# Half of a similarity matrix by transposes, and a second image prepared at another time: an attention and scan kernel on one Trainium2 core

## The chip, the cores and the metric

The kernel runs on one core of a Trainium2 chip. The time is device microseconds of one execution; the time of a version is the median of its runs. The core has five engines that work through queues of their own: PE (TensorE, matrix products; "PEld" is its weight load), DVE (VectorE), ACT (ScalarE), POOL (GpSimd) and SP (SyncE, which here only issues transfers). They wait for one another by semaphores. An engine takes its instructions in order, so an instruction that waits holds up all that stand behind it.

## What is computed

Eight images x of 256 channels and 48 x 48 = 2304 positions go through two layers. Each layer normalizes its input in groups of eight channels (`_gn`), and the result is added to the input.

```python
# layer 0
feat_pos = tokens @ W.T + bias
feat = feat_pos[:, :, :c]
pos = feat_pos[:, :, c:]
...
pos = pos / jnp.maximum(norm, 1e-12)
sim = jnp.einsum('bnc,bmc->bnm', pos, pos)
topksim, topkid = jax.lax.top_k(sim, K)
topkfeat = jax.vmap(lambda f, idx: f[idx])(feat, topkid)
attn = jax.nn.softmax(topksim, axis=-1)
out = jnp.einsum('bnk,bnkc->bnc', attn, topkfeat)
```

K is 16. The matrix sim (2304 x 2304 for each image) is symmetric. Layer 1 is a state-space model, twice in a row (DEPTH = 2): a layer norm, a projection, a convolution of four taps, SiLU, step sizes by softplus, and the recurrence

```python
dA = jnp.exp(dt_t[:, :, None] * A)
h = h * dA + dt_t[:, :, None] * B_t[:, None, :] * x_t[:, :, None]
y = jnp.einsum('bds,bs->bd', h, C_t)
```

over all 2304 positions, for 512 inner channels and 16 states, then a gate and a projection back.

## The kernel before

**Two streams.** Layer 0 of an image is a Python generator, `layer0` (L230 to L522), that issues a little work and then yields. Layer 1 is one long list of slots (L991 to L1008). The first image's layer 0 runs alone (L528); the Tile framework may reorder instructions there. From `manual_schedule` (L545) on, the order of issue is the order of the program. There, each slot m issues its share of layer 1 and then calls `ahead.go(m)` (L1008, L977), which takes one step of the next image's `layer0`. So image 1's layer 0 runs beside image 0's layer 1, and so on; the last image's layer 1 has no company.

**Layer 1.** A unit is one chunk of 384 positions at one depth; an image has 12 units, and a unit has 32 slots, so an image has 384. A slot holds one scan step: ACT makes decays (`decay`, L820, one slot ahead), POOL products `bx` (`make_bx`, L797, for two slots), DVE the scan (`run_scan`, L832), and DVE or POOL the product with C. Two hand-made tables, `between` and `behind` (L929, L943), give the slot, relative to the unit's first scan, of all else: for instance `load_v` at -42, `affine` and `mean` at -37, `center` at -35, `normal` at -22 (it makes vn), `in_proj` 0 at -21, `x_proj` at -13. Entries of `between` are issued before the slot's scan, those of `behind` after it. The slots begin at -42. `load_v` of an image first calls `ahead.finish` (L971), which issues whatever is left of that image's layer 0 in one piece; image 1's `load_v` is in slot 12 x 32 - 42 = 342.

**Layer 0.** First statistics: six chunks xs of x are loaded (L251, L264), DVE makes `bn_stats` (L261), and `group_stats` (L182) turns these into rstd and shift in eight steps, through PE, ACT and POOL. The weights w0 (512 KB) are loaded after the first chunks (L255). Then each chunk is loaded a second time (xt, L267 and L278), ACT normalizes it (L280), PE projects it (pp, L310, to pos; pf, L319, to feat), and pos is scaled by its inverse norm. Then come 18 blocks of 128 rows, by the table `within` (L500), 16 steps apart: `similar` (L394, five pieces psim of up to 512 columns, each two matmuls), `keep_similar` (L404, ACT copies them to sim), `top` (L410, DVE: maximum of eight, replace, maximum, replace), `others` (L432, ACT: rest), `turn` (L439, PE transposes sim and subtracts the rest), `weights` (L451, ACT: exp, aT), `weigh` (L459, PE: po), `average` (L469, ACT: o), `turn_back` (L478, PE: pr), `finish` (L486, DVE adds x and makes statistics; x1 is stored). `within` starts at -9 and its last step is 17 x 16 + 24 = 296, so there are 306 steps, and eight more of `group_stats`. Before its first block the generator yields `begin`, which is -9 (L515). `go` then waits until `(m + 1 - PHASE - begun) % BLOCK == 0` (L986, PHASE 6, BLOCK 16), so that image 1's blocks keep a fixed phase against layer 1's slots.

**Constants.** ACT issues 28 small loads at the start (L121 to L152) and then takes the exp of A_sb (L153). After image 0's layer 0, DVE makes the diagonal matrices dg of D_param (L540), and they are stored to memory (L541), for `load_d` (L687).

Of the kernel before, what the change touches and what calls it, by code (L numbers as in the profile page):

```python
# [8 lines left out]
F32 = mybir.dt.float32  # L9
BF16 = mybir.dt.bfloat16  # L10
AF = mybir.ActivationFunctionType
# [4 lines left out]
P = 128  # L16
# [9 lines left out]
def tile_conv_preact(  # L26
# [41 lines left out]
    BLOCK = 16  # L68
    TOPK = (1, 10)
    PHASE = 6  # L70


    SHARE = ("GGVGGGVVGGGGGGVG", "GGGVGVVGVVVGVGVG", "VGVGVGVVGGVVGGVG")
# [62 lines left out]
    for d in range(DEPTH):  # L136
        xp = xp_wT[d].rearrange("(k p) e -> p k e", p=P)

        nc.scalar.dma_start(xp_sb[:, d, :, d * RB : d * RB + R], xp[:, :, 0:R])
        nc.scalar.dma_start(xp_sb[:, d, :, R - d * R : E - d * R], xp[:, :, R:E])  # L140
        nc.scalar.dma_start(dtp_sb[d * RB : d * RB + R, :], dtp_wT[d])
        nc.scalar.dma_start(nw[:, d], norm_w[d].rearrange("(k p) -> p k", p=P))
        nc.scalar.dma_start(nbias[:, d], norm_b[d].rearrange("(k p) -> p k", p=P))
        nc.scalar.dma_start(cw[:, d], conv_w[d].rearrange("(k p) t -> p k t", p=P))
        nc.scalar.dma_start(cbias[:, d], conv_b[d].rearrange("(k p) -> p k", p=P))
        nc.scalar.dma_start(dtb[:, d], dtp_b[d].rearrange("(k p) -> p k", p=P))
        nc.scalar.dma_start(dpar[:, d], D_param[d].rearrange("(k p) -> p k", p=P))
        for j in range(J):
            nc.scalar.dma_start(
                A_sb[j * G : (j + 1) * G, d],  # L150
                A_log[d].rearrange("(i g) s -> g i s", g=G)[:, :, j * Q : (j + 1) * Q],
            )  # L152
    nc.scalar.activation(A_sb, A_sb, AF.Exp)  # L153

    nc.vector.tensor_scalar(A_sb, A_sb, LEAST, -1.0, ALU.max, ALU.mult)

    h_st = const.tile([P, DEPTH, STEPS, Q], F32, tag="h_st", name="h_st")
    tail = const.tile([P, DEPTH, CB, H], F32, tag="tail", name="tail")

    def rsqrt_start(r, var, eps):  # L160

# [20 lines left out]
    def group_stats(st, found, mm0, name):  # L182


        mv = small.tile([P, CB, 2], F32, tag="gn_mv", name=f"mv_{name}")
        for cb in range(CB):
            nc.vector.bn_aggr(mv[:, cb, :], st[:, cb])
# [5 lines left out]
        nc.scalar.copy(mean, pm)  # L193
# [18 lines left out]
        nc.gpsimd.tensor_scalar(shift, shift, -1.0, None, ALU.mult)  # L212
        found.extend((rstd, shift))
        yield
# [12 lines left out]

    def layer0(b, left, pool, ps0, alone):  # L230
        def mm0(w, name):
            return ps0.tile([P, 512], F32, tag="mm", name=name, bufs=5 if alone else 3)[:, :w]
# [11 lines left out]
        def leave_psum():  # L244
# [1 line left out]
                made, use = pending.pop(0)  # L246
                use(made)

        st = small.tile([P, CB, NCH, 6], F32, tag="gn_st0", name=f"st0_{b}")
        xs = {  # L250
            c: load_chunk(pool, x[b], c, "x", f"xs_{b}_{c}", 3 * more) for c in range(2 * more)  # L251
        }
# [5 lines left out]
        for c in range(NCH):  # L258
            xt = xs.pop(c)
            for cb in range(CB):  # L260
                nc.vector.bn_stats(st[:, cb, c, :], xt[:, cb, :])  # L261
            n = c + 2 * more
            if n < NCH:
                xs[n] = load_chunk(pool, x[b], n, "x", f"xs_{b}_{n}", 3 * more)  # L264
            yield
        found = []
        nxt = load_chunk(pool, x[b], 0, "x", f"xt_{b}_0", 3 * more)  # L267
        yield from group_stats(st, found, mm0, f"a{b}")
        rstd, shift = found
        pos = pool.tile([P, CB, N], F32, tag="pos", name=f"pos_{b}", bufs=1)  # L270
        feat = pool.tile([P, NB, C], F32, tag="feat", name=f"feat_{b}", bufs=1)
        loaded = {0: nxt}
        n2, rn = {}, {}

        def normalized(c):
            xn = loaded.pop(c)
            if c + 1 < NCH:
                loaded[c + 1] = load_chunk(pool, x[b], c + 1, "x", f"xt_{b}_{c + 1}", 3 * more)  # L278
            for cb in range(CB):
                nc.scalar.activation(  # L280
                    xn[:, cb, :], xn[:, cb, :], AF.Identity,
                    bias=shift[:, cb : cb + 1], scale=rstd[:, cb : cb + 1],
                )
            return xn
# [106 lines left out]
        PT = 4  # L391
        blocks = [{} for _ in range(NB)]

        def similar(t, i):  # L394

            c0, w = widths[i]
            pm = blocks[t]["psim", i] = mm0(w, f"psim_{b}_{t}_{i}")
            for k in range(CB):
                nc.tensor.matmul(  # L399
                    pm, pos[:, k, t * P : (t + 1) * P], pos[:, k, c0 : c0 + w],  # L400
                    start=(k == 0), stop=(k == CB - 1),
                )

        def keep_similar(t, i):  # L404
            c0, w = widths[i]
            if i == 0:
                blocks[t]["sim"] = pool.tile([P, N], F32, tag="sim", name=f"sim_{b}_{t}", bufs=2)
            nc.scalar.copy(blocks[t]["sim"][:, c0 : c0 + w], blocks[t].pop(("psim", i)))  # L408

        def top(t, i):  # L410

# [110 lines left out]
        left.update(x1=x1, rstd=found[0], shift=found[1])  # L522

    lefts = [{} for _ in range(B)]
    with tc.tile_pool(name="first", bufs=1) as pool0, tc.tile_pool(
        name="first_ps", bufs=1, space=PSUM
    ) as ps0:
        for _ in layer0(0, lefts[0], pool0, ps0, True):  # L528
            pass

    diag = hbm.tile([P, DEPTH, DC + 1, DB, P], F32, tag="diag", name="diag", bufs=1)
    with tc.tile_pool(name="setup", bufs=2) as setup:
        for d in range(DEPTH):
            for t in range(DC, DC + 1):
                dg = setup.tile([P, DB, P], F32, tag="dg", name=f"dg_{d}_{t}")
                for k in range(DB):
                    f = cw[:, d, k, t : t + 1] if t < DC else dpar[:, d, k : k + 1]
                    nc.vector.tensor_scalar(dg[:, k], ident, f, None, ALU.mult)  # L540
                nc.sync.dma_start(diag[:, d, t], dg)  # L541
# [144 lines left out]

    def load_d(unit, k):  # L687
        unit["dmat"][k] = keep.tile([P, P], F32, tag="dmat", name=f"dmat_{unit['u']}_{k}")
        nc.sync.dma_start(unit["dmat"][k], diag[:, unit["d"], DC, k])

    def tap(unit, e):
        d = unit["d"]
# [267 lines left out]
    class Ahead:  # L960
# [26 lines left out]

# [62 lines left out]
```

## Time and profile before

| what | us |
|---|---|
| runs | 9895.0 to 9908.42, median of 4: 9903.97 |
| the profiled execution | 9895.45 |
| its span | 9893.7 |
| first MAX8 (top) of image 0 | 88.3 |
| last block's MAX8 of image 0 | 415.3 |
| first scan (slot 0) | 521.4 |
| first scan of the last image | 8819.7 |

Over the span DVE is busy for 8958.5 us (91%), POOL for 8943.4 (90%), PE for 8001.0 (81%) and ACT for 7326.8 (74%). These shares mix stages with different limits, so they are read by stage. In the profile's group lines stand the line of the kernel, the engine, the operation, the tile written and the tiles read, and the shape; in a timeline, the start and the duration come first, and in square brackets the idle time of the engine before the instruction and what ended it. "SPq" and "ACTq" are issues of transfers. Matmul records overlap, because PE is pipelined; the distance of their starts is what one costs.

### The profile page before, as it was taken

What the parts mean: (1) busy time and instruction counts of PE and PEld (TensorE: products, weight loads), DVE (VectorE), ACT (ScalarE), POOL (GpSimd) and SP (SyncE); (2) the same over time, 40 slices, a digit from 0 to 9 for tenths busy, and PEclk for the clock granted to TensorE, in tenths of its full rate; (3) what the DMA queues carried; (4) which work ended last, traced back from release to release, by engine and by line L of the source; (5) the groups of instructions that cost most, each with busy time, mean ns of one, the idle gap of its engine ahead of it and who ended that gap; (6) DMA issues with size and microseconds to landing.
All of it is one profiled execution on the core that took longest, in us unless ns stands there. A gap on an engine that the chain in (4) does not pass through costs nothing. (4 is left out here: it accounts for less than half of the span.)

```text
span 9893.7 us, 133780 instructions
## 1 busy us (share of the span) xinstructions
PE 8001.0 (81%) x36736; PEld 4381.5 (44%) x36736; DVE 8958.5 (91%) x7993; ACT 7326.8 (74%) x15966; POOL 8943.4 (90%) x3927
## 2 busy tenths in 40 slices
PE   8888887788878888788877888788887788866665
PEld 6644544444534454344444445344544444422222
DVE  4589998999989999899998999889998999988998
ACT  4477787778777877777777787777777778766766
POOL 0089999999989999899998999999998999999999
PEclk9989998899988998899988999889998899977777
DMA  1144445444444444544454444444445444444544
GB/s 32 37 132 124 137 129 152 123 131 128 137 137 134 126 139 132 144 121 140 126 151 126 134 125 138 142 133 122 137 126 155 119 135 126 140 136 130 144 140 121
DMA packets 1243503, 1271.37 MB, mean 129 GB/s; under 512 B 266592, under 2 KB 1215840, under 8 KB 1242752
## 3 DMA queue, kind: packets, MB, share of 16 engines
q1 hardware_dynamic: 1230496, 1262.45, 45.1%
q8 instruction: 293, 4.80, 0.2%
q14 instruction: 458, 3.75, 0.1%
q10 hardware_dynamic: 12256, 0.36, 0.1%
HBM read 1048.94 MB, written 212.86 MB: 128 GB/s over the span
## 5 line engine op out<-in xcount | busy, mean ns | idle before, releaser
L804 POOL TENSOR_TENSOR bx<-BC,dtxr 128x1536 f32<-128x1536 f32 x1536 | 5304.3, 3457 | 115.6 <-PE y L889 56.0
L828 ACT ACTIVATE da<-dtr,A_sb 128x385 f32<-128x385 f32 x6144 | 3594.9, 585 | 867.7 <-DVE bx L843 558.9
L843 DVE TENSOR_TENSOR_SCAN bx<-da,bx 128x770 f32<-128x770 f32 x2040 | 3523.6, 1747 | 188.3 <-ACT da L828 140.9
L871 POOL TENSOR_TENSOR bx<-bx,BC 128x1536 f32<-128x1536 f32 (+1 forms) x1320 | 3308.8, 2507 | 213.7 <-DVE bx L843 203.6
L843 DVE TENSOR_TENSOR_SCAN da<-da,bx 128x770 f32<-128x770 f32 x1032 | 1809.3, 1753 | 189.4 <-ACT da L828 144.6
L602 PE MATMUL pe<-vn,inw 128*128 128x384 f32 (+1 forms) x3072 | 1249.9, 539 | 393.5 <-DVE xr L924 87.7
L399 PE MATMUL psim<-pos 128*128 128x512 f32 (+1 forms) x2880 | 1371.0, 608 | 182.2 <-ACT sim L408 75.2
L465 PE MATMUL po<-feat,aT 128*128 128x256 f32 x5184 | 1362.2, 412 | 14.4 <-ACT aT L454 7.5
L889 PE MATMUL y<-bx,sel 128*32 128x384 f32 x12288 | 1226.7, 534 | 44.4 <-POOL bx L871 33.9
L465 PEld LDWEIGHTS po<-feat,aT 128*128 128x128 f32 x5184 | 1027.1, 205 | 362.0 <-issue 112.1
L845 DVE TENSOR_TENSOR bx<-da,BC 128x768 f32<-128x768 f32 x1032 | 989.2, 958 | 35.5
L602 PEld LDWEIGHTS pe<-vn,inw 128*128 128x128 f32 x3072 | 585.6, 205 | 902.6 <-issue 184.0
L399 PEld LDWEIGHTS psim<-pos 128*128 128x128 f32 x2880 | 552.7, 206 | 817.4 <-issue 468.2
L889 PEld LDWEIGHTS y<-bx,sel 128*32 128x32 f32 x12288 | 394.8, 118 | 862.4 <-issue 734.4
L702 DVE SCALAR_TENSOR_TENSOR xc<-pe,cw,xc 128x384 f32<-128x384 f32 x1152 | 696.4, 611 | 43.1 <-ACT xc L694 15.9
L732 PE MATMUL pd<-dbl,dtp_sb 16*128 16x384 f32 x768 | 426.9, 672 | 338.2 <-ACT dt L741 206.1
L859 ACT COPY h_st<-da 128x2 f32<-128x2 f32 x832 | 131.8, 158 | 685.4 <-DVE bx L845 679.3
L454 ACT ACTIVATE aT<-pt 128x512 f32<-128x512 f32 (+1 forms) x720 | 388.4, 549 | 246.7 <-PE pt L446 240.4
L445 PE MATMUL pt<-ident,sim 128*128 128x128 f32 x2592 | 538.0, 290 | 38.9 <-DVE v L666 22.1
L907 PE MATMUL pw<-z,ow 128*128 128x384 f32 x1536 | 527.9, 496 | 14.2 <-DVE v L666 7.5
L437 ACT ACTIVATE rest<-left,three 128x512 bf16<-128x512 f32 (+1 forms) x720 | 467.2, 671 | 59.4 <-DVE left L422 59.4
L446 PE MATMUL pt<-minus,rest 128*128 128x128 bf16 x2592 | 489.9, 224 | 3.3 <-ACT rest L437 3.2
(146 smaller groups left out, 9777.8 us busy)
## 6 DMA issues: line engine op xcount, KB each, us to landing
dtxr<-dtx_d SPq DMA_DIRECT2D x6144, 48.0 KB, 1.8
dtr<-dt_d SPq DMA_DIRECT2D x6144, 48.0 KB, 1.8
BC<-bc_d SPq DMA_DIRECT2D x768, 192.0 KB, 3.8
inw<-in_in_wT_dram SPq DMA_DIRECT2D x768, 128.0 KB, 2.2
dtx_d<-dtx SPq DMA_DIRECT2D x384, 192.0 KB, 2.0
dt_d<-dt SPq DMA_DIRECT2D x384, 192.0 KB, 2.2
ow<-in_out_wT_dram SPq DMA_DIRECT2D x96, 512.0 KB, 3.9
dmat<-diag SPq DMA_DIRECT2D x384, 64.0 KB, 2.3
```

What stands on the lines that cost most here:

```text
L399: nc.tensor.matmul(pm, pos[:, k, t * P : (t + 1) * P], pos[:, k, c0 : c0 + w], start=(k == 0), stop=(k == CB - 1),)
L445: nc.tensor.transpose(pt[:, q], row["sim"][:, r], ident)
L465: nc.tensor.matmul(row["po"], aT[:, m % PT, :], feat[:, m, :], start=(m == 0), stop=(m == NB - 1))
L602: nc.tensor.matmul(pe, w[:, k], unit["vn"][:, k, lo:], start=(k == 0), stop=(k == CB - 1))
L702: nc.vector.scalar_tensor_tensor(unit["xc"][e], unit["pe"][e][:, k : k + T], cw[:, unit["d"], e, k : k + 1], unit["xc"][e], ALU.mult, ALU.add,
L804: nc.gpsimd.tensor_tensor(bx[:, :, 1:], unit["BC"][0], unit["dtxr"][i].unsqueeze(1).to_broadcast([P, Q, T]), ALU.mult,)
L828: nc.scalar.activation(da[:, s * (1 + T) : (s + 1) * (1 + T)], unit["dtr"][i], AF.Exp, scale=A_sb[:, unit["d"], i, p * HQ + s : p * HQ + s ...
L843: nc.vector.tensor_tensor_scan(h, da, g, 0.0, ALU.mult, ALU.add)
L845: nc.vector.tensor_tensor(bx[:, :, 0:T], da.rearrange("p (q t) -> p q t", q=HQ)[:, :, 1:], unit["BC"][1][:, qs], ALU.mult,)
L871: nc.gpsimd.tensor_tensor(g[:, :, 0:T], g[:, :, 1:], unit["BC"][1][:, qs], ALU.mult)
L889: nc.tensor.matmul(y[j * G : (j + 1) * G, :], sel, unit["bx"][k * J + j][:, q, 0:T], start=False, stop=True, skip_group_check=True,)
L907: nc.tensor.matmul(pw, unit["ow"][:, k, cb * P : (cb + 1) * P], unit["z"][k], start=(k == 0), stop=(k == DB - 1),)
```

## The change

- **Similarities of image 0** (`alone`): for row block t, column blocks left of the diagonal are no longer multiplied. `keep_similar` also has POOL copy the part right of the diagonal into a new tile `tri`; `similar` transposes the copies of rows m < t into place and multiplies only from the diagonal on. The other images multiply as before.
- **Constants**: their 26 loads go from ACT's queue to SP's, and are issued after image 0's group statistics and the load of w0. The exp of A_sb and the matrices dg follow there, ahead of the first normalization in program order. The separate stage that made dg after layer 0 is gone.
- **Input chunks of image 0** are all loaded at once, kept in six buffers, and not loaded a second time.
- **Image 1's input statistics** are made during image 0's blocks, one step every fourth slot. Its layer 0 then starts in slot -20 (`EARLY`) instead of -42, and has fewer steps: it lacks the 14 of the statistics.
- **Images 2 to 7**: w0 is loaded ahead of the first two chunks rather than after them; the first second load of x is issued after the statistics, one step ahead of its normalization, and there is one step more before the blocks.

```diff
+    EARLY = -20
...
-        nc.scalar.dma_start(xp_sb[:, d, :, d * RB : d * RB + R], xp[:, :, 0:R])
...
+    def scan_constants():
+        for d in range(DEPTH):
...
+            nc.sync.dma_start(xp_sb[:, d, :, d * RB : d * RB + R], xp[:, :, 0:R])
...
+        nc.scalar.activation(A_sb, A_sb, AF.Exp)
+
+        nc.vector.tensor_scalar(A_sb, A_sb, LEAST, -1.0, ALU.max, ALU.mult)
...
+    known = {}
+
+    def input_stats(b, pool, mm0, ahead, kept):
+        bufs = NCH if kept is not None else 3
+        st = small.tile([P, CB, NCH, 6], F32, tag="gn_st0", name=f"st0_{b}")
+        xs = {c: load_chunk(pool, x[b], c, "x", f"xs_{b}_{c}", bufs) for c in range(ahead)}
+        yield
+        for c in range(NCH):
+            xt = xs.pop(c)
+            for cb in range(CB):
+                nc.vector.bn_stats(st[:, cb, c, :], xt[:, cb, :])
+            n = c + ahead
+            if n < NCH:
+                xs[n] = load_chunk(pool, x[b], n, "x", f"xs_{b}_{n}", bufs)
+            if kept is not None:
+                kept[c] = xt
+            yield
+        found = []
+        yield from group_stats(st, found, mm0, f"a{b}")
+        known[b] = found
...
+        if alone:
+            loaded = {}
+            yield from input_stats(b, pool, mm0, 6, loaded)
+        else:
+            loaded = {0: None}
         w0_t = pool.tile([P, N], F32, tag="left", name=f"w0_{b}", bufs=more)
         w0_sb = w0_t[:, 0 : CB * 2 * C].rearrange("p (k o) -> p k o", k=CB)
         nc.sync.dma_start(w0_sb, w0T.rearrange("(k p) o -> p k o", p=P))
...
+        if not alone:
+            if b not in known:
+                yield from input_stats(b, pool, mm0, 2, None)
+            loaded[0] = load_chunk(pool, x[b], 0, "x", f"xt_{b}_0", 3)
+        yield
+        rstd, shift = known[b]
...
+        if alone:
+            tri = pool.tile([P, NB * (NB - 1) // 2 * P], F32, tag="tri", name="tri", bufs=1)
+
+        def above(t, m, n):
+            at = t * NB - t * (t + 1) // 2 + m - t - 1
+            return tri[:, at * P : (at + n) * P]
+
         def similar(t, i):
 
             c0, w = widths[i]
             pm = blocks[t]["psim", i] = mm0(w, f"psim_{b}_{t}_{i}")
+            if alone:
+                for m in range(c0 // P, min(t, (c0 + w) // P)):
+                    nc.tensor.transpose(pm[:, m * P - c0 : (m + 1) * P - c0], above(m, t, 1), ident)
+                lo = max(c0, t * P)
+                if lo < c0 + w:
+                    for k in range(CB):
+                        nc.tensor.matmul(
+                            pm[:, lo - c0 :], pos[:, k, t * P : (t + 1) * P], pos[:, k, lo : c0 + w],
+                            start=(k == 0), stop=(k == CB - 1),
+                        )
+                return
...
             nc.scalar.copy(blocks[t]["sim"][:, c0 : c0 + w], blocks[t].pop(("psim", i)))
+            lo = max(c0, (t + 1) * P)
+            if alone and lo < c0 + w:
+                nc.gpsimd.tensor_copy(
+                    above(t, lo // P, (c0 + w - lo) // P), blocks[t]["sim"][:, lo : c0 + w]
+                )
...
         yield begin
+        other = input_stats(1, pool, mm0, 6, {}) if alone and B > 1 else iter(())
         for m in range(begin, max(parts) + 1):
+            if m >= 0 and m % 4 == 0:
+                next(other, 0)
...
+        run = layer0(0, lefts[0], pool0, ps0, True)
+        while 0 not in known:
+            next(run)
+        scan_constants()
+        for d in range(DEPTH):
+            dg = pool0.tile([P, DB, P], F32, tag="dg", name=f"dg_{d}", bufs=1)
+            for k in range(DB):
+                nc.vector.tensor_scalar(dg[:, k], ident, dpar[:, d, k : k + 1], None, ALU.mult)
+            nc.sync.dma_start(diag[:, d], dg)
+        for _ in run:
             pass
...
         def go(self, m):
-            if self.image == B:
+            if self.image == B or m < EARLY:
                 return
```

More of the change, by code (lines that the diff above doesn't have):

```diff
@@ L135, in tile_conv_preact @@
     A_sb = const.tile([P, DEPTH, STEPS, Q], F32, tag="A_sb", name="A_sb")
-    for d in range(DEPTH):
-        xp = xp_wT[d].rearrange("(k p) e -> p k e", p=P)
-        nc.scalar.dma_start(xp_sb[:, d, :, d * RB : d * RB + R], xp[:, :, 0:R])
[L140 to L152, printed above, removed]
@@ L153, in tile_conv_preact @@
-    nc.scalar.activation(A_sb, A_sb, AF.Exp)
-    nc.vector.tensor_scalar(A_sb, A_sb, LEAST, -1.0, ALU.max, ALU.mult)
     h_st = const.tile([P, DEPTH, STEPS, Q], F32, tag="h_st", name="h_st")
     tail = const.tile([P, DEPTH, CB, H], F32, tag="tail", name="tail")
+    def scan_constants():
+        for d in range(DEPTH):
+            xp = xp_wT[d].rearrange("(k p) e -> p k e", p=P)
+            nc.sync.dma_start(xp_sb[:, d, :, d * RB : d * RB + R], xp[:, :, 0:R])
+            nc.sync.dma_start(xp_sb[:, d, :, R - d * R : E - d * R], xp[:, :, R:E])
+            nc.sync.dma_start(dtp_sb[d * RB : d * RB + R, :], dtp_wT[d])
+            nc.sync.dma_start(nw[:, d], norm_w[d].rearrange("(k p) -> p k", p=P))
+            nc.sync.dma_start(nbias[:, d], norm_b[d].rearrange("(k p) -> p k", p=P))
+            nc.sync.dma_start(cw[:, d], conv_w[d].rearrange("(k p) t -> p k t", p=P))
+            nc.sync.dma_start(cbias[:, d], conv_b[d].rearrange("(k p) -> p k", p=P))
+            nc.sync.dma_start(dtb[:, d], dtp_b[d].rearrange("(k p) -> p k", p=P))
+            nc.sync.dma_start(dpar[:, d], D_param[d].rearrange("(k p) -> p k", p=P))
+            for j in range(J):
+                nc.sync.dma_start(
+                    A_sb[j * G : (j + 1) * G, d],
+                    A_log[d].rearrange("(i g) s -> g i s", g=G)[:, :, j * Q : (j + 1) * Q],
+                )
+        nc.scalar.activation(A_sb, A_sb, AF.Exp)
+        nc.vector.tensor_scalar(A_sb, A_sb, LEAST, -1.0, ALU.max, ALU.mult)
@@ L247, in leave_psum @@
                 use(made)
[L249 to L252, printed above, removed]
+        if alone:
[3 more added lines that the diff above has]
+            loaded = {0: None}
         w0_t = pool.tile([P, N], F32, tag="left", name=f"w0_{b}", bufs=more)
@@ L256, in layer0 @@
         sq = w0_t[:, CB * 2 * C : CB * 2 * C + CB * T].rearrange("p (k t) -> p k t", k=CB)
+        if not alone:
+            if b not in known:
+                yield from input_stats(b, pool, mm0, 2, None)
+            loaded[0] = load_chunk(pool, x[b], 0, "x", f"xt_{b}_0", 3)
         yield
[L258 to L269, printed above, removed]
+        rstd, shift = known[b]
         pos = pool.tile([P, CB, N], F32, tag="pos", name=f"pos_{b}", bufs=1)
         feat = pool.tile([P, NB, C], F32, tag="feat", name=f"feat_{b}", bufs=1)
-        loaded = {0: nxt}
         n2, rn = {}, {}
@@ L276, in normalized @@
             xn = loaded.pop(c)
-            if c + 1 < NCH:
-                loaded[c + 1] = load_chunk(pool, x[b], c + 1, "x", f"xt_{b}_{c + 1}", 3 * more)
+            if not alone and c + 1 < NCH:
+                loaded[c + 1] = load_chunk(pool, x[b], c + 1, "x", f"xt_{b}_{c + 1}", 3)
             for cb in range(CB):
@@ L408, in keep_similar @@
             nc.scalar.copy(blocks[t]["sim"][:, c0 : c0 + w], blocks[t].pop(("psim", i)))
+            lo = max(c0, (t + 1) * P)
+            if alone and lo < c0 + w:
+                nc.gpsimd.tensor_copy(
+                    above(t, lo // P, (c0 + w - lo) // P), blocks[t]["sim"][:, lo : c0 + w]
+                )
         def top(t, i):
@@ L524, in tile_conv_preact @@
     lefts = [{} for _ in range(B)]
+    diag = hbm.tile([P, DEPTH, DB, P], F32, tag="diag", name="diag", bufs=1)
     with tc.tile_pool(name="first", bufs=1) as pool0, tc.tile_pool(
@@ L527, in tile_conv_preact @@
     ) as ps0:
-        for _ in layer0(0, lefts[0], pool0, ps0, True):
-            pass
[L533 to L541, printed above, removed]
+        run = layer0(0, lefts[0], pool0, ps0, True)
[8 more added lines that the diff above has]
+        for _ in run:
+            pass
     keep = ctx.enter_context(tc.tile_pool(name="keep", bufs=2))
@@ L688, in load_d @@
         unit["dmat"][k] = keep.tile([P, P], F32, tag="dmat", name=f"dmat_{unit['u']}_{k}")
-        nc.sync.dma_start(unit["dmat"][k], diag[:, unit["d"], DC, k])
+        nc.sync.dma_start(unit["dmat"][k], diag[:, unit["d"], k])
     def tap(unit, e):
```

## The prediction

> **What bounds the kernel now.** I read the page's slices first, then the busy time by stage, then single stretches of the timeline.
>
> ```profile
> PE   8888887788878888788877888788887788866665
> DVE  4589998999989999899998999889998999988998
> POOL 0089999999989999899998999999998999999999
> ```
>
> A digit is 247 us. The first slice and most of the second are the first image's layer 0 alone: PE is full, POOL empty, DVE half used. From the third slice DVE and POOL are the two full engines. The stages confirm it; columns are PE, PEld, DVE, ACT, POOL, clock, DMA:
>
> ```profile
> 300.00:400.00 100.00, 98.93 (x481) 68.73 (x479) 58.86 (x56) 45.10 (x91) 0.00 (x0) 1.00 0.05 14
> 600.00:700.00 100.00, 76.02 (x325) 36.77 (x319) 97.29 (x79) 75.32 (x169) 98.09 (x40) 0.85 0.47 131
> ```
>
> So work taken from PE or ACT counts before some 440 us; after it, only what stops DVE or POOL counts. The stage alone looks like a pure PE limit, but one row block in the timeline shows a ring as tight as PE:
>
> ```profile
> 245.40 2.54 DVE L422 MATCH_REPLACE8 left<-top,left 128x2304 f32<-128x2304 f32 x1
> ...
> 247.97 1.95 ACT L437 ACTIVATE rest<-left,three 128x512 bf16<-128x512 f32 x3 [1.56 <-DVE left L422]
> 249.82 0.46 ACT L472 ACTIVATE o<-po,den 128x256 f32<-128x256 f32 x1
> 250.33 0.44 PE L482 MATMUL pr<-ident,o 128*128 128x128 f32 x2
> 250.61 6.18 PE L399 MATMUL psim<-pos 128*128 128x512 f32 x16
> 256.82 0.37 ACT L408 COPY sim<-psim 128x256 f32<-128x256 f32 x1 [0.28 <-PE psim L399]
> 257.23 2.56 DVE L415 MAX8 top<-sim 128x8 f32<-128x2304 f32 x1 [5.42 <-ACT sim L408]
> ```
>
> DVE's four passes end at 247.94; ACT then makes rest and o, PE turns o back, computes the next block's similarities, ACT copies them, DVE starts again: 19.76 us, the same from block 2 to block 17 (118.93 to 415.30).
>
> **Similarities.** Before, each of the 18 blocks makes 18 column blocks of 128 by two matmuls in two passes each; a 512-wide pass starts every 0.43 us, so a column block costs 4 x 0.43 / 4 = 0.43. Block t now has t of them transposed. Transposes of one kind stand back to back once (95.42, five of them), with weight loads of 0.142 us, so I take 0.14; bounds are 0.11 (a transpose and its bf16 partner start 0.17 apart, the partner 0.06) and the record's full 0.28. Block t saves 0.29t of PE.
>
> What is late next? If o is still turned back ahead of the last four pieces (2304 - 512 columns), only columns past 512 shorten the ring: blocks 5 to 16 save 0.29 x (1+...+12) = 22.6, and block 17 some 3.4, 26 together. If the scheduler lifts similarities over that wait, PE's own time counts, until ACT holds it: 10.5 of DVE, 1.95 rest, 0.45 o, 0.2 exp, 0.6 rest, five copies and the last rest 2.7, or 16.4 a block, 3.4 under 19.76. Blocks 2 to 11 then give 0.29 x 65 = 18.9 and six give 3.4 each, 39 together. Block 1 gives nothing (DVE is late there: 88.30 to 98.68 is its own four passes). The 17 sets of copies on POOL are covered by an empty engine: 19584 columns, at 3457 ns for 1536 in POOL's two-input multiply at most 44 us over 330. A transpose that waits for its copy would hold all of PE's queue, but the freshest copy it needs was due a whole block period earlier. Second-image statistics put twelve bn_stats of 0.51 us into DVE; those due between the last passes are in the ring, about 2 us, the rest falls into DVE's 5.42 us wait; their six loads pass only the small xr loads on SP. Between 26 and 39 less 2 I take **31**; with 0.28 a transpose it would be 13, the lower bound.
>
> [...]
>
> **Start.**
>
> ```profile
> 15.68 0.47 DVE L187 BATCH_NORM_AGGREGATE mv_a<-st 128x2 f32<-128x36 f32 x2
> 21.68 4.41 ACTq L149 DMA_DIRECT2D A_sb<-in_A_log_dram  x4
> 26.13 0.16 ACT L193 COPY mean_a<-pm_a 128x2 f32<-128x2 f32 x1 [24.05 <-DMA A_sb<-in_A_log_dram]
> 30.34 3.10 ACT L280 ACTIVATE xt<-xt,shift_a,rstd_a 128x384 f32<-128x384 f32 x5 [0.44 <-POOL shift_a L212]
> ```
>
> The mean is ready at 16.9 but ACT issues constants until 26.09. With these on SP the last chunk is issued at about 0.8 + 6 x 1.13 = 7.6, lands near 11, statistics end at 12.5, and the chain of 4.2 us (26.13 to 30.34) plus matrix product ends at 17.4: 13 us gained. But the 26 constants took ACT's queue 24 us (1.86 to 26.09); on SP, behind six chunks and w, they would end near 26 to 33, and the exp of A_sb is queued on ACT among the first normalizations, with all of ACT's work behind it. If it stands ahead of them, the 13 are lost and up to 3 more (33 against 30.34). Between -3 and 13 I take **7**. The chunks' second load vanishes, at no gain: ACT never waited for it. dg's eight passes (1.67 us) now sit in DVE's empty 16 to 47 us.
>
> **Hand-over to the scans.**
>
> ```profile
> 448.31 0.37 SPq L613 DMA_DIRECT2D v<-x  x1
> 461.27 1.02 DVE L261 BATCH_NORM_STATS2 st<-xs 128x6 f32<-128x384 f32 x2 [1.04 <-DMA xs<-in_x_dram]
> 462.21 0.94 DVE L636 TENSOR_TENSOR v<-v,lm 128x768 f32<-128x768 f32 x1
> 477.83 1.31 ACT L679 ACTIVATE vn<-v,nbias,nw 128x384 f32<-128x384 f32 x2
> ```
>
> v waited for dg's write, then 3.3 us for landing; the mean's matmuls ended at 455.35, but centering stood behind bn_stats of image 1 until 462.21; vn stood behind image 1's pos and feat. Without all that: affine at 448.6 (shift at 448.56) instead of 451.66, center 452.4, then this unit's own durations to vn at about 461 instead of 477.8, 16 us. PE's granted clock is 0.50 to 0.54 until some 477, so in_proj and x_proj now fall into half speed, 2 to 8 us lost. I take **14**, bounds 8 and 18.
>
> **Image 1 comes late.** Its 50th step, which returns the begin of the blocks, comes at slot -20 + 49 = 29. Blocks start where (slot + 4) is a multiple of 16: before, the 64th step came at 21 and blocks started after 28; now 29 misses 28 and waits for 44. Of 314 steps only 297 have run when slot 342 calls finish, which issues the other 17 in one piece ahead of load_v and of scan 342. Nine are the last block's weights and products, eight the statistics. Queued behind them: on DVE the scan, on ACT decay 344, on POOL the next products. In the first image the same tail, from weigh at 430.01 to the aggregate's end at 443.96, is 14 us; some 3 of it can run before DVE arrives, so I take **11** lost, bounds 7 and 18. The freed slots give nothing back: POOL stays full there.
>
> **Every later image** now issues w ahead of its first chunks.
>
> ```profile
> 1577.93 1.02 DVE L261 BATCH_NORM_STATS2 st<-xs 128x6 f32<-128x384 f32 x2 [5.21 <-DMA xs<-in_x_dram]
> ```
>
> The second chunk landed 6.2 us after its issue at 1572.70, w (512 KB) 7.6 after 1573.21, so w took the last 1.9. If transfers go in order, the first chunk, and DVE, wait up to 1.9 longer in each of six images; if they share, 0.5 for the issue. I take 7 of 0 to 14. The first reload of x is now issued one slot (3 us) ahead of its use, and these loads land in 3.4 to 4.8: up to 1 us of ACT six times, **2**. Image 1's chunk work after slot 0 adds **2** more (0 to 4).
> [...]
>
> **Sum.** Gained 31 + 7 + 14 = 52; lost 11 + 7 + 2 + 2 = 22; net 30. The profiled execution took 9895.45 us (span 9893.70 and 1.75 around it), giving 9865; the median of the runs, 9903.97, is 8.5 above it, so I forecast 9874.
>
> **Rivals.**
> - *All bounds good* (0.14): similarities run ahead (39 - 2), the start gives 13, no piled-up end: net 50, 9854. For it: PSUM has five buffers for them. Against: ACT's order.
> - *The ring stays* (0.16): transposes cost 0.28 or o's turn holds PE; 13 instead of 31: net 12, 9892. For it: the constant 19.76 with DVE waiting 5.42.
> - *Constants block ACT* (0.09): the exp waits for late loads, start gives -3: net 20, 9884.
> - *Slower* (0.08): at the start of each of images 2 to 7, DVE waits for the whole of w and ACT's decays wait behind a reload not landed. w's 8 us landing and 1.4 for a chunk, 0.5 issue, less 5.7 is 4.2, a full reload 3.7: 7.9 x 6 = 47 instead of 9. Net -8, 9912. It decides from 39 / 6 = 6.5 us per image. For it: DVE waits there already. Against: ACT has slack, one slot lies between.
>
> **Chances.** The forecast has 0.53, own range 9862 to 9886. Within 0.2% (20 us) is what a measurement of this kernel can't tell from no change. Faster: 0.50 of the forecast, 0.14, and 0.03 of the third rival, 0.67. Slower: 0.06, of the last and of a wrong end. The rest, 0.27, is the same. The range 9850 to 9900 leaves out the last rival and the ends of two others.
>
> **What would show it.** Block periods falling from 19.76 to under 17; normalization first at 18 to 25; vn some 14 us sooner after the last block's statistics than the 477.83 - 442.45 = 35.4 of before; a DVE gap of some 11 us at image 1's load_v; DVE waits of 6 to 7 us for xs in images 2 to 7. Constant periods, or waits over 10 us there, would prove me wrong.

## The result and the profile after

After the change the kernel takes 9914.53 us (median of 42 runs, 9904.56 to 9926.33) against 9898.99 us (60 runs, 9887.93 to 9909.21) of the kernel before: a ratio of 1.0015, with a 95% interval from 1.0010 to 1.0019. It is 16 us slower, where 9874 and a gain were forecast. The span of its profiled execution is 9911.6 us, 17.9 longer than before's 9893.7.

The slices of DVE and POOL on the changed kernel's page, each 248 us wide, look nearly as before:

```profile
DVE  5589997999989999899988999889998999988998
POOL 1199997999989999899998999899998999999999
```

Apart from single digits that are one or two higher or lower, only the first slices differ: POOL now works there, on its copies. The 18 us are not to be seen in tenths, so I read where fixed points of the program lie in both traces:

| stretch | before, us | after, us | difference |
|---|---|---|---|
| start to the first normalization | 30.34 | 17.15 | -13.2 |
| from there to the first MAX8 | 58.0 | 58.3 | +0.4 |
| first to last block's MAX8 of image 0 | 327.0 | 303.5 | -23.5 |
| last MAX8 to the first scan (slot 0) | 106.1 | 87.4 | -18.7 |
| **all up to slot 0** | 521.4 | 466.4 | **-55.0** |
| slots 0 to 384 (scans of image 0) | 1182.1 | 1215.8 | +33.7 |
| slots 384 to 2688 (images 1 to 6) | 7116.2 | 7156.1 | +39.9 |
| last image to the end | 1074.0 | 1073.3 | -0.7 |

The gains were forecast at 52 and are 55. The losses were forecast at 22 and are 73.6. Image 2's preparation begins at slot 342, so the first of the six later images counts in the row of slots 0 to 384, and the last in the row of slots 384 to 2688.

**The blocks.** One block in the timeline of the changed kernel, to be laid beside the block of before:

```profile
237.36 1.94 ACT L476 ACTIVATE rest<-left,three 128x512 bf16<-128x512 f32 x3 [1.09 <-DVE left L461]
239.21 0.45 ACT L511 ACTIVATE o<-po,den 128x256 f32<-128x256 f32 x1
...
239.72 0.44 PE L521 MATMUL pr<-ident,o 128*128 128x128 f32 x2 [1.01 <-ACT o L511]
...
239.99 0.71 PE L423 MATMUL psim<-ident,tri 128*128 128x128 f32 x5
...
240.54 4.04 PE L427 MATMUL psim<-pos 128*128 128x384 f32 x12
...
244.61 0.37 ACT L442 COPY sim<-psim 128x256 f32<-128x256 f32 x1 [0.28 <-PE psim L427]
245.02 2.56 DVE L454 MAX8 top<-sim 128x8 f32<-128x2304 f32 x1 [3.82 <-ACT sim L442]
```

From the turn of o (239.72) on it is the same ring as before. PE even stands still ahead of that turn for 1.01 us, waiting for ACT's o. What shrank is the work behind it: five transposes and 4.04 us of products where 6.18 us of products stood. The periods say the same: 7.73 and 28.32 us, then 19.76, 19.76, 19.44, 19.12, 18.81, and so on down to 15.91 and 15.76. From the fifth block on each is some 0.32 shorter than the last. That is the price of one column block: the products of a column block cost 0.43 us, and transposes here start 0.11 us apart (0.109 to 0.115 in all 123 pairs that stand next to one another).

**Slot 342**, on DVE, in the changed kernel:

```profile
1525.71 0.96 DVE L885 TENSOR_TENSOR bx<-da,BC 128x768 f32<-128x768 f32 x1
1539.29 0.35 DVE L530 SCALAR_TENSOR_TENSOR xr<-pr,b_feat,xr 128x128 f32<-128x128 f32 x1 [12.62 <-PE pr L521]
...
1552.98 1.02 DVE L242 BATCH_NORM_STATS2 st<-xs 128x6 f32<-128x384 f32 x2 [7.11 <-DMA xs<-in_x_dram]
```

The first bracket is the pile-up: DVE stands for 12.62 us while the last block of image 1 goes through PE and ACT in one piece. POOL's idle time ahead of its first statistics step there is 13.8 us. The second bracket is image 2's first chunk behind w: 7.11 us, 5.21 before.

**Images 2 to 7.** Waits of ACT and of DVE from 1400 to 9000 us in the changed kernel (us in total, times, longest):

```profile
ACT pos L353 <- PE pp L326: 79.5, 30, 3.8
ACT feat L362 <- PE pf L335: 52.6, 30, 3.6
ACT xt L296 <- DMA xt<-in_x_dram: 23.1, 6, 4.1
DVE st L242 <- DMA xs<-in_x_dram: 42.2, 6, 8.2
```

Before, the first two were 48.0 and 2.9, ACT's normalization never waited for a load (it waited for shift, 33.1 in six), and DVE waited 31.2 for xs. So three things are seen: the chunk now waits 1.8 us longer in each of six images, ACT waits 3.9 for each reload, and the projections reach ACT at a worse time. The wait for the reload is not all new. It has taken the place of a longer one for shift, 33.1 before against 23.1 now.

### The profile page after: what moved, and what is told of

It is laid out like the page before. It is cut to its first block, busy times and chain, and to the rows that moved or that the text cites. A ratio compares the mean times of both kernels' runs of the same rounds, so it can differ in the third digit from the quotient of the medians.

```text
span 9911.6 us, 133908 instructions
## 1 busy us (share of the span) xinstructions
PE 7997.9 (81%) x36761; PEld 4392.5 (44%) x36761; DVE 8963.9 (90%) x7993; ACT 7322.9 (74%) x15966; POOL 8970.0 (90%) x3980
## 5 line engine op out<-in xcount | busy, mean ns | idle before, releaser
L433 PE MATMUL psim<-pos 128*128 128x512 f32 x2520 | 1224.4, 617 | 193.3 <-ACT sim L442 75.9
L433 PEld LDWEIGHTS psim<-pos 128*128 128x128 f32 x2520 | 485.6, 207 | 769.8 <-issue 414.9
L926 PE MATMUL y<-xc,dmat 128*128 128x384 f32 x768 | 398.5, 606 | 118.7 <-DVE xc L742 79.4
```

Of the source, the lines that this page charges most:

```text
L433: nc.tensor.matmul(pm, pos[:, k, t * P : (t + 1) * P], pos[:, k, c0 : c0 + w], start=(k == 0), stop=(k == CB - 1),)
```

## Experiments

The theory after these readings: the gains came in sum as sized, and three places of layer 1 take back more than all of them: the pile-up at slot 342, the late reload, and the order of w. The rival: the losses are one general slowing of the interleaved part (POOL's copies, DMA traffic, moved phases), which undoing single edits doesn't cure. Each experiment changes only order or time of issue unless its diff shows more, and computes the whole result. Differences between kernels are of medians; those of one group shared a chip. The kernel before stood at 9901.83, 9899.90, 9899.08 and 9899.06 in the four groups, so the groups may be compared to some 3 us. By the spread of the runs, a difference between two kernels of experiments 1 to 4 is known to some 3 to 8 us (95%), and one with a kernel of four or five runs to some 6 to 14. A difference of 4 us is therefore not told from none.

### 1. Image 1 one slot earlier

```diff
-    EARLY = -20
+    EARLY = -21
```

> One number is changed in the changed kernel: EARLY is -21 instead of -20, so image 1's layer 0 starts one slot sooner and its blocks should start after slot 28 instead of 44. Theory (image 1 comes late by one slot, and the end of its layer 0 is issued in one piece): DVE's 12.6 us wait at image 1's load_v goes, units 10 and 11 of image 0 return from 122.8 and 103.7 us towards 100, and the time falls by 20 to 27 us against the changed kernel (9914.5), to about 9890. Rival (units 10 and 11 are long because of the new order of loads of image 2, and the waiting only moves): under 8 us.

Measured: 9890.0 us (11 runs; ratio to before 0.9990, interval 0.9981 to 0.9999), 24.5 less than after. By the starts of the scans, the last two units of image 0 take 103.5 and 103.4 us instead of 122.8 and 103.7. Image 1's first MAX8 comes at 578.8 us instead of 634.3, which is the 16 slots. So the missed phase costs about twice what DVE's visible wait of 12.62 says. The busy time by window tells why, for unit 10 (slots 320 to 352) of the changed kernel and then of this one; columns are PE, PEld, DVE, ACT, POOL, clock, DMA share, GB/s:

```profile
1455.70:1578.50 122.80, 85.38 (x388) 48.60 (x386) 100.27 (x105) 75.04 (x173) 89.98 (x46) 0.78 0.46 133
1449.50:1553.00 103.50, 67.68 (x302) 34.02 (x300) 89.30 (x93) 67.70 (x157) 89.88 (x46) 0.76 0.56 154
```

Of the 19.3 us, 11.0 are work of DVE. The last block's four passes (2.55 each) stand in this unit only when image 1 comes late. The other 8.3 are idle time of DVE. Units 0 and 1, which have one block less, take 196.1 us against 196.4: the time saved there is nothing. The span of the two profiled executions also differs by 4.0 us ahead of slot 0, where their programs are the same; that part is chance.

### 2 to 4. The later images, undone step by step

From the changed kernel: the reload goes ahead of `group_stats` (xt_early); then the added step goes as well (xt_early_no_step); then w also returns to its place behind the first two chunks (later_as_before, whose diff is shown).

```diff
-            yield from input_stats(b, pool, mm0, 2, None)
-            loaded[0] = load_chunk(pool, x[b], 0, "x", f"xt_{b}_0", 3)
-        yield
+            yield from input_stats(b, pool, mm0, 2, None, load_w0, load_xt0)
...
+        if first is not None:
+            first()
         yield
...
+        if then is not None:
+            then()
         yield from group_stats(st, found, mm0, f"a{b}")
```

> The changed kernel with one thing undone for images 2 to 7: the first reload of x (xt 0) is issued ahead of group_stats, as before, and not one step ahead of its normalization; the added step stays, and w0 stays ahead of the first chunks. Theory A (ACT's 4.0 us wait for xt is what costs): about 4 x 6 = 24 us less than the changed kernel. Theory B (the chunk steps come one slot later against layer 1's tables, and that misfit costs): under 6 us less.

> As xt_early, and without the added step, so that for images 2 to 7 the chunk steps stand in the same slots as before; only w0 stays ahead of the first chunks. Theory A (the wait for xt costs): the same as xt_early within 5 us. Theory B (the slot costs): 20 to 30 us less than xt_early. Under both some 10 us stay lost to w0 ahead of xs (1.9 us for each of six images).

> As xt_early_no_step, and w0 is loaded after the first two chunks again, so images 2 to 7 issue what they did before; image 0 and image 1 stay as in the changed kernel. By the order of transfers in one queue: 9 to 12 us less than xt_early_no_step, and 35 to 45 us less than the changed kernel in all. If transfers share the engines evenly: under 3 us less than xt_early_no_step.

Measured: 9891.29 (11 runs; 0.9989, 0.9980 to 0.9997), 9887.4 (11 runs; 0.9986, 0.9977 to 0.9995) and 9867.97 (6 runs; 0.9965, 0.9953 to 0.9978). By medians the steps are worth 23, 4 and 19 us, 46.5 together. That the reload's 23 equals ACT's wait of 23.1 is a coincidence: with the early reload and the added step, ACT still waits 11.4 us for shift at the same place, so only 11.7 us of its wait go. The step looked worth little, yet its mark left the trace: the waits for pp and pf fell from 92.0 and 49.3 (xt_early) to 51.3 and 6.3. The order of w took 8.5 us off DVE's waits for xs (39.4 to 30.9), and twice that off the time, more than the 9 to 12 expected.

### 5 and 6. Both undone, and then without the transposes

`both` is later_as_before with EARLY = -21. `both_all_products` multiplies all columns again and has no `tri`:

```diff
-            if alone:
-                for m in range(c0 // P, min(t, (c0 + w) // P)):
-                    nc.tensor.transpose(pm[:, m * P - c0 : (m + 1) * P - c0], above(m, t, 1), ident)
...
-            lo = max(c0, (t + 1) * P)
-            if alone and lo < c0 + w:
-                nc.gpsimd.tensor_copy(
...
```

> later_as_before and early21 together: image 0's stage as in the changed kernel, image 1 from slot -21, images 2 to 7 as before. If the two losses are separate, 24 us below later_as_before (9868), about 9843, some 58 us under the kernel before. If the pile-up at slot 342 and the later images' starts are one and the same loss, 9860 or more.

> The kernel 'both' with image 0 multiplying all similarities again (no transposes, no copies on POOL). If o's turn ahead of the similarities holds the block period (the ring), the transposes are worth 22 to 29 us and this is that much slower than 'both'; if PE alone held it, 35 to 44.

Measured: 9849.66 (5 runs; 0.9948, 0.9936 to 0.9961) and 9875.47 (10 runs; 0.9975, 0.9966 to 0.9984). The two losses separate: alone they are 24.5 and 46.5, together 64.9, and the 6 us between that and their sum are within the noise. Without transposes the periods are 19.76 again, and first to last MAX8 takes 327.0. The transposes are worth 25.8 us by medians and 24.9 by these two stretches: the ring's size, not PE's.

### 7. The turn of o four steps later

If the ring is what bounds the blocks, taking o's turn out of it must shorten the early blocks, too, in which transposes bring nothing.

```diff
-            (-5, similar, 4), (-8, keep_similar, 0), (-5, keep_similar, 2), (24, turn_back), (18, weigh, 1),
+            (-5, similar, 4), (-8, keep_similar, 0), (-5, keep_similar, 2), (28 if alone else 24, turn_back), (18, weigh, 1),
...
-            (19, weigh, 2), (20, weights, 4), (21, weigh, 4), (24, finish),
+            (19, weigh, 2), (20, weights, 4), (21, weigh, 4), (28 if alone else 24, finish),
```

> The kernel 'both' with turn_back and finish of image 0's blocks moved from step 24 to step 28, so that o's turn stands behind the next block's similarities and no longer ahead of them. By the ring the first periods (19.75) should fall to 17 to 18.5 and the sum of image 0's blocks by 8 to 15 us. If PE holds the period, it stays within 2 us.

Measured: 9826.9 (5 runs; 0.9927, 0.9914 to 0.9941), 22.8 less than `both`, with runs from 9812 to 9838. The periods are 18.52 where they were 19.75, and 15.75 for the last six; first to last MAX8 takes 283.8 us, 18.3 less, also more than the 8 to 15 expected. A block of it in the timeline:

```profile
240.32 1.33 ACT L493 ACTIVATE rest<-left,three 128x512 bf16<-128x512 f32 x2 [1.59 <-DVE left L478]
240.79 0.57 PEld L440 LDWEIGHTS psim<-ident,tri 128*128 128x128 f32 x4
...
241.56 0.45 ACT L528 ACTIVATE o<-po,den 128x256 f32<-128x256 f32 x1
...
244.88 0.38 PE L538 MATMUL pr<-ident,o 128*128 128x128 f32 x2
...
246.22 2.54 DVE L471 MAX8 top<-sim 128x8 f32<-128x2304 f32 x1
```

The similarities (240.79) now start before ACT has made o (241.56), and o is turned (244.88) when they are through. MAX8 doesn't wait for them: what stands ahead of it on DVE is the sum with pr, which starts at 245.30 after DVE has waited 2.29 us for pr. The view of busy time by window, for 200 to 300 us (PE, PEld, DVE, ACT, POOL, clock, DMA share, GB/s), first of the changed kernel:

```profile
200.00:300.00 100.00, 92.05 (x527) 71.43 (x526) 61.29 (x62) 50.63 (x104) 7.79 (x16) 1.00 0.06 17
```

and then of this one:

```profile
200.00:300.00 100.00, 99.23 (x587) 80.29 (x586) 70.93 (x68) 51.19 (x109) 6.68 (x15) 1.00 0.06 17
```

The change had left PE with 8% of idle time, because the ring and not PE held the block; without the ring's knot PE is full again, and has 60 matmul records more in the same 100 us.

### 8. Image 1 from slot -42 again

```diff
-    EARLY = -21
+    EARLY = -42
```

> The kernel 'both' with EARLY at -42: image 1's statistics are still made ahead, but its chunk work starts with the slots, as before, and its blocks start after slot 12 instead of 28. If the hand-over was shortened mainly because statistics and their loads are out of the way, within 5 us of 'both'. If the late start is what shortened it, the first scan comes 8 to 14 us later again and the time rises by as much.

Measured: 9871.81 (8 runs; 0.9973, 0.9963 to 0.9983), 22 more than `both`: more than either theory. The time from the last MAX8 to slot 0 is 104.2 us, against 87.3 in `both` and 106.1 before; vn comes 61.2 us after the last MAX8, against 45.3 and 62.5. The two profiled spans differ by 17.1 us, of which 16.9 lie there. So nearly the whole hand-over gain comes from image 1's later start, whose pos and feat no longer stand ahead of vn. Statistics and dg out of the way are worth some 2 us of it.

### 9 to 11. The later images' edits, one by one

On the version of experiment 7, run again as the base: w ahead of the chunks alone, and then the late reload with its added step.

```diff
+            load_w0()
-            yield from input_stats(b, pool, mm0, 2, None, load_w0, load_xt0)
+            yield from input_stats(b, pool, mm0, 2, None, None, load_xt0)
```

```diff
-            yield from input_stats(b, pool, mm0, 2, None, load_w0, load_xt0)
+            yield from input_stats(b, pool, mm0, 2, None, load_w0, None)
+            load_xt0()
+            yield
```

> The version with start -21, the later images as before, and the step that turns o back moved from 24 to 28, once more, as the base of the two runs beside it. Expected 9820 to 9835 (9826.9 the first time).

> As the base, but in images 2 to 7 w0 is again loaded ahead of the first two chunks. Theory A, from the traces of the earlier pair (8.5 us less wait of DVE for xs, 6 of the span): it costs 6 to 10 us, so 9833 to 9837, and the wait of DVE for xs in images 2 to 7 rises by 8 to 9 us. Theory B, from the medians of the earlier pair: 17 to 21 us, so 9844 to 9848, more than DVE's wait, because the delay reaches POOL and the products as well.

> As the base, but in images 2 to 7 the first chunk's second load is again issued after the statistics, one step ahead of its normalization, with the step that this adds. Theory A: ACT waits some 4 us in each of six images and all of it is passed on, 23 us, with 0 to 4 for the added step: 9850 to 9854. Theory B: part of the earlier 23 us came from the image 1 pile-up behind which all stood; without it less than 15 us are left, 9842 or less.

Measured: the base 9822.99 (4 runs; 0.9921, 0.9908 to 0.9935). With w first 9850.97 (5 runs; 0.9945, 0.9931 to 0.9958), 28 more, nearer to theory B, although DVE waits only 8.2 us longer for xs (40.1 against 31.9). With the late reload and its step 9870.66 (5 runs; 0.9967, 0.9955 to 0.9980), 47.7 more, about twice the 23 to 27 of theory A; neither theory foresaw it.

### 12 and 13. The step and the late reload apart

```diff
             yield from input_stats(b, pool, mm0, 2, None, load_w0, load_xt0)
+            yield
```

```diff
-        yield from group_stats(st, found, mm0, f"a{b}")
+        for n, _ in enumerate(group_stats(st, found, mm0, f"a{b}")):
+            if n == 7 and then is not None:
+                then()
+            yield
```

> As the base (turn_later_again), but with the added step between the statistics and the first normalization in images 2 to 7; the reload stays early. Late reload and added step together cost 41 us between the first scans of images 1 and 7 here. Theory A, the reload is the larger part: the step alone costs 0 to 12 us, so 9823 to 9835. Theory B, the step costs at least as much as the wait, because it moves the chunks' projections against layer 1's slots (the scans lose 6 us at once around slot 0 of each image): 17 to 25 us, so 9840 to 9848.

> As the base, but the first chunk's second load is issued one slot ahead of its normalization, without the added step. Theory A: ACT waits some 4 us six times and passes it on, 18 to 30 us, so 9841 to 9853. Theory B: the wait alone costs half or less of that, 5 to 15 us, so 9828 to 9838, because ACT catches up within the image.

Measured: 9837.81 (5 runs; 0.9938, 0.9925 to 0.9950) and 9837.05 (5 runs; 0.9937, 0.9924 to 0.9951). Each alone costs 14 to 15 us: the step between its two theories, the reload at the upper end of theory B (5 to 15). Together they cost 47.7, more than their sum. The waits of ACT in the kernel with the step alone:

```profile
ACT pos L371 <- PE pp L344: 82.6, 30, 3.9
ACT feat L380 <- PE pf L353: 50.9, 29, 3.3
ACT xt L314 <- POOL shift_a L214: 11.5, 6, 1.9
```

and in the kernel with the late reload alone:

```profile
ACT pos L371 <- PE pp L344: 52.5, 24, 3.6
ACT xt L314 <- DMA xt<-in_x_dram: 18.6, 3, 6.6
ACT xt L314 <- POOL shift_a L214: 16.6, 3, 5.5
ACT feat L380 <- PE pf L353: 6.6, 10, 1.0
```

The first shows where the waits for pp and pf of the changed kernel come from: the step alone brings them (pos and feat 133.5 us, against 52.6 in the base). The second shows that the late reload alone hardly makes ACT wait longer. Without the step, ACT waits for shift anyway: 33.1 us in the base, and here 35.2, half of it now put down to the load. With the step the wait for shift is down to 11.5, and the load's takes its place. That makes the sum larger than its parts plausible; it does not give its size, and waits of ACT are no measure of the price: the step alone adds 81 us to those for pp and pf, takes 22 from that for shift, and costs 15.

The price can be read in one place: the stretch from slot 342 of an image to 60 slots later, in which the next image's layer 0 begins. The loss is in it six times, and behind it the images hardly grow further. Sums over the six stretches, us:

| kernel | time | DVE idle | of it ahead of scans |
|---|---|---|---|
| before | 1201.5 | 217.2 | 112.6 |
| changed | 1252.4 | 264.0 | 147.3 |
| xt_early | 1232.8 | 244.7 | 130.3 |
| xt_early_no_step | 1222.4 | 237.9 | 124.2 |
| later_as_before | 1204.1 | 219.7 | 114.8 |
| base (turn_later_again) | 1204.8 | 220.6 | 116.3 |
| base, step alone | 1216.7 | 228.6 | 127.4 |
| base, late reload alone | 1213.5 | 228.3 | 123.7 |
| base, late reload and step | 1251.9 | 262.9 | 154.9 |
| base, w first | 1226.6 | 241.3 | 126.9 |

Here the changed kernel's loss splits into 20 for the reload, 10 for the step and 18 for w, 48 together. For reload and w that is nearly all idle time of DVE, for the step two thirds. For reload and step most of that idle time stands ahead of scans; for w, by the base and its version, 8.2 is DVE's own stop for xs and 10.6 stands ahead of scans. These are single executions, but the six images mostly agree. With the medians, the reload is worth 9 to 14 alone, 20 to 23 in the changed kernel and 33 to 35 on top of the step; the step 4 to 15; w 18 to 28. Their sum in the changed kernel, 46.5 to 48, is sharp.

## Why the prediction was wrong

**The gains: right in sum, with two sizes and one reason off.**

- *Start*: 13.2 instead of 7. These rows of the changed kernel show the good end of my bounds:

```profile
11.72 0.47 DVE L189 BATCH_NORM_AGGREGATE mv_a<-st 128x2 f32<-128x36 f32 x2
...
12.94 0.16 ACT L195 COPY mean_a<-pm_a 128x2 f32<-128x2 f32 x1 [10.86 <-PE pm_a L192]
...
17.15 1.30 ACT L296 ACTIVATE xs<-xs,shift_a,rstd_a 128x384 f32<-128x384 f32 x2 [1.76 <-POOL shift_a L214]
```

  I had 17.4. The rival in which the exp of A_sb blocks ACT did not come: ACT runs it at 32.92 us, behind the first normalizations, and does not stand for it.
- *Similarities*: 23.5 by the trace, 25.8 by experiment 6, instead of 31. Of the two cases that I had put 31 between, the lower held (26): "o is still turned back ahead of the last four pieces", so "only columns past 512 shorten the ring". The transposes' price of 0.14 was too high: they start 0.11 us apart, the lower bound, so a column block saves 0.32, and 0.32 x (1+...+12) + 4.0 for the last block gives 29. The trace's size is lower because the first two periods lost 5.4 us (7.73 and 28.32 against 10.38 and 20.24): MAX8 and the first replace of block 1 stand on DVE ahead of and behind block 0's last pass (83.19 to 88.24), and rest of block 0 begins only at 88.29. PE stands for 5.8 us until then, and its granted clock is 0.50 from 89 to 95 us (0.98 over 80 to 100 before). The order of issue in this stage is the scheduler's; why it swapped them was not tried.
- *Hand-over*: 18.7 instead of 14, the top of the bounds, but I named the statistics in front of the centering and the write of dg as well as image 1's pos and feat. Experiment 8 shows that the last are nearly all of it.

**The losses: every place was named, and the sizes failed.**

- *Image 1 comes late*: 11 predicted, 24.5 measured. The miss of phase by one slot, the 17 left steps, and DVE's stop (12.62) came as worked out. The step that failed is the price: I took the stop at slot 342 for the whole of it. What the later start also did was to push the blocks back by 16 slots, so that a block's four passes, 10 us of DVE, fell into unit 10, where DVE is busy for 89.3 of 103.5 us without them (experiment 1; with them the unit takes 122.8). "The freed slots give nothing back" was right, and was the reason that this work cost its whole length; I put it at nothing.
- *Late reload*: 2 predicted, 20 to 23 measured with the added step, 9 to 14 without it. The failed step is "issued one slot (3 us) ahead of its use", from which "up to 1 us of ACT six times" followed. The timeline of the changed kernel at image 2:

```profile
1594.25 0.40 SPq L83 DMA_DIRECT2D xt<-in_x_dram  x1
...
1595.79 0.22 POOL L214 TENSOR_SCALAR shift_a<-shift_a 128x2 f32<-128x2 f32 x1
...
1597.97 1.30 ACT L296 ACTIVATE xt<-xt,shift_a,rstd_a 128x384 f32<-128x384 f32 x2 [3.83 <-DMA xt<-in_x_dram]
...
1600.45 1.77 DVE L883 TENSOR_TENSOR_SCAN da<-da,bx 128x770 f32<-128x770 f32 x1 [2.87 <-issue]
```

  ACT had stood at the normalization since 1597.97 - 3.83 = 1594.14, before SP issued the load at 1594.25. A slot in the program is not a slot on the clock for every engine: ACT had run ahead of SP by the whole slot, and waited for the whole landing, 3.7 us. Up to 1596.01 it would have waited for shift in any case, so the load adds 1.9. DVE stands 2.87 us ahead of a scan right after, 0.94 with the early reload (xt_early); but before the change it stood 2.54 there, too, behind ACT's wait for shift. So the wait itself, 11.7 us in six images, is half of the price; that the rest is DVE's idle time ahead of the scans is seen, and the instruction that hands it on stays open.
- *The added step*: I priced the step of the program not at all. It is worth 4 to 15 us. It shifts the projections against layer 1's table, and ACT waits 81 us more for PE and 22 less for shift; that the price comes from this shift is likely, not shown.
- *w ahead of xs*: 7 predicted, of 0 to 14; 18 to 28 measured, of which DVE's wait is 8. The price of the wait itself was right. The wait was not the whole cost: about as much again (10.6 in the base's version) is idle time of DVE ahead of scans, and which instruction passes it on stays open.
- *Image 1's chunk work after slot 0*: 2 predicted. With both losses undone, slots 0 to 384 still take 6.7 us more than before (1188.8), and chunk work is one part of that.

**The rivals.** "Slower" named the right place, DVE waiting for w and ACT for the reload, at a price of 47, and undoing those edits with the added step gave 46.5. Its waits were not what it had: 1.8 us per image for w, not 4.2, and 3.9 for the reload, not 3.7, of which half stood there without it; the step and what follows the waits made up the rest. I gave it 0.08 because "ACT has slack, one slot lies between". The slot between was none on the clock, and whether ACT has slack no run tells. That its total, 9912, lies near 9914.5 is partly luck: it priced the losses at 11 + 47 + 2 = 60 where 73.6 came, and the gains at 52 where 55 came, from a median that was 5 us higher. One rival was added up wrongly: "All bounds good" gives 37 + 13 + 14 less 11, which is 53 and not 50.

**The granted clock and the order of transfers.** The granted clock is 1.00 in the blocks with the most transposes (the rows of 200 to 300 us above, and 300 to 370 in the changed kernel), so no run here shows a loss by the clock in them. The 0.50 at 89 to 95 us came after PE had stood for 5.8 us; the first transpose of similarities starts later, at 100.0. For w the forecast's 7 stood between two cases: transfers in order, 1.9 us in each of six images or 11 together, and shared, 0.5 each or 3 together. DVE's wait grew by 11.0 in the changed kernel, 42.2 less 31.2, where the other edits had a part, too. With w's place alone changed it grew by 8.5 and 8.2, between the two cases. The price in time, 18 to 28, is larger than either.

## What to carry to other kernels

In a hand-made interleaving, price a moved step by what is queued behind it and by where its work falls, not by the wait that it shows: here a wait of 12.6 us was worth 24.5, one of 8 was worth 18 to 28, and one step without work up to 15. When a start is held to a phase, count the slot in which it arrives; one slot too late cost a full turn of 16. And before counting what an engine is relieved of, follow the ring through all engines: PE at 99% did not set the period, for the first blocks with transposes kept 19.76 us with less work on PE. Once the transposes had made room on PE, moving the turn of o behind the similarities gave 22.8 us, nearly as much as they had. With the losses undone and this added, the changed kernel takes 9826.9 us, and 9822.99 in its repetition, less than both kernels.

## What the hardware did that I had not expected

- Six loads of 384 KB were issued by SP within 3.31 us, 0.55 each, not the 1.13 that I took; the last statistics were aggregated at 11.72 us.
- A copy of 512 columns on POOL took 0.61 us, of 256 columns 0.40. The transposes' weight loads, which read these copies, stood idle for 0.2 us in all between 80 and 380 us: no copy was late.
- The similarities' transposes of 128 x 128 stayed 0.11 us apart in every block, up to 13 in a row among products, with 1.00 of the clock granted from 100 to 379 us. The profile's record of one is 0.27 long.
- Delays in an image's preparation need not add: late reload and added step cost 14 and 15 us alone and 47.7 together. Two executions of one kernel (experiment 7 and its repetition) differ by up to 3.5 us between the same slots of an image, so a single image is no evidence for sizes of this kind.
